# Head 0 of a patch-attention kernel: where its 1x1 results are written, in which order its units run, and when its keys are read

## The chip, the core and the metric

The kernel runs on one core of a Trainium2 chip. The metric is the device time of one execution in microseconds (us). TensorE is called PE here (PEld is its weight load), VectorE DVE, ScalarE ACT, GpSimd POOL and SyncE SP. DMAs are issued from three queues: SP's, ACT's and POOL's.

## The reference

An image x of 48 channels and 256 x 256 pixels goes through two layers. What matters here is the first part of the first layer.

```
x = x + L0(gn(x));  x = x + L1(gn(x))        # gn: group norm over 16 groups of 3 channels
L0(v):
    qkv = einsum('bchw,oc->bohw', v, w_qkv)   # 1x1 convolution, 48 -> 144 channels
    qkv = dwconv3x3(qkv, w_dw)                # each channel alone, 3x3 taps
    q, k, v = heads(unfold(split(qkv)))       # 4x4 patches (padding 4): 8 heads of 96 rows x 4356 patches
    q, k = l2norm(q), l2norm(k)               # over the 96 rows
    attn = softmax((q^T k) * temperature)     # 4356 x 4356 for each head
    out = w_proj @ fold(v @ attn)
```

The patches that lie in the padding are zero, so 4096 patches are computed and the others enter the softmax sum as a constant. L1 is a sum of three separable transforms over 64 x 64 windows; nothing of it is changed.

## The kernel before

Data flow of the first 260 us. The whole image is read into one tile `xr` (128 partitions, 128 rows of 256 pixels: the upper and lower half of the image in partitions 0 to 63 and 64 to 127). `bn_stats` on DVE and `group_stats` give the group norm, which is folded into the 1x1 weights `wq` (heads 0 and 1) and `wr` (heads 2 to 7) and a bias.

*1x1 results.* `mix(n)` (L626 on) computes the 1x1 convolution of heads 0 and 1, which have 36 channels, for four rows in each quarter of the image: 2 PSUM tiles of 1024 columns, each by 4 products on PE, moved out by ACT or DVE into one of four `oi` tiles that are 258 pixels wide with a zero at each end. Two DMAs, one on SP's queue and one on POOL's, store the 36 channels of both heads to the DRAM tensor `t1[0]`, whose rows are 258 wide. There are 16 such calls: 8 before the units, the other 8 between them (the table `behind`).

*Units.* A `Banded` unit is a quarter of the image rows (b = 0 to 3) for one of head 0's keys, queries and values (z = 1, 0, 2, in this order), so 12 units. Each does:

- `load`: 6 DMAs on SP's queue read its rows of `t1[0]`, with two rows of overlap, into a pad tile.
- `taps`: 6 products on PE with a banded matrix give the 3x3 convolution, in one PSUM tile of 96 x 1024.
- for keys and queries: `square` (ACT, from PSUM), `reduce` (DVE), `norm` (a product on PE), `root` (DVE, ACT, DVE), `scale` (DVE, from PSUM), `high` (ACT rounds to fp32r), `low` (DVE, the remainder), and two stores of 384 KB to the DRAM tensor `qkv0`, on ACT's and POOL's queues.
- for values: `copy` (ACT) and one store on ACT's queue.

The pads and the results lie in parts of `xr` whose pixels are no longer needed (`spare`). The order on every engine is the written one (`manual_schedule`): while unit k's first three products run, unit k-1 is normalised and scaled; only then come `high` of k-1, the other three products of k, `low` of k-1, `square` and `reduce` of k.

*Branch and keys.* Then comes `tc.If(large > 0)` (L717), whose body computes exact row maxima for large temperatures. With these inputs it is jumped over, and at its end SP waits for all DMAs that are under way. After it, the first queries and all 8 key tiles of head 0 (512 KB each, in four DMAs) are loaded over the three queues, then two value tiles. Attention (L477 logits, L804 exponentials, L838 weighted sums) follows; it works off head after head, while the units of the next head run beside it, and takes most of the time. Keys and queries are held as two fp32r parts, so a logits tile takes three products.

In the built program each DMA waits for the one that used its semaphore before: eight semaphores go round for POOL's queue, and eight for SP's and ACT's together.

Of the kernel before, what the change touches and what calls it, by code (L numbers as in the profile page):

```python
# [55 lines left out]
def conv_preact_kernel(  # L56
# [60 lines left out]
    early_only = taps.enter_context(tc.tile_pool(name="diag", bufs=1))  # L117
# [347 lines left out]
    def load_queries(qt, h, g):  # L465
        col = g * 256, (g + 1) * 256
        to = qt.bitcast(F32)
        for i in range(2):
            load(to[0:HD, i, :], h, i, 0, *col)
            load(to[HD:128, i, :], h, i, 0, *col, nc.sync, 0, 32)  # L470
            load(to[i * 64 : (i + 1) * 64, 2, :], h, i, 0, *col, nc.sync, 32)
# [26 lines left out]
    class Banded:  # L498


        def __init__(self, b, z, pad, spare):
            self.b, self.z, self.pad, self.spare = b, z, pad, spare

        def load(self):
            rows = t1[0][self.z * HE : (self.z + 1) * HE]
            for q in range(4):
                y = q * QR + self.b * BR
                nc.sync.dma_start(
                    out=self.pad[0 : BR * HE, q, :], in_=rows[:, y : y + BR, :].rearrange("c y x -> y c x")
                )  # L510
            for y in range(BR, BR + 2):
                y0 = self.b * BR + y
                nc.sync.dma_start(out=self.pad[y * HE : (y + 1) * HE], in_=rows[:, y0 : y0 + 3 * QR + 1 : QR, :])

        def taps(self, pool, half):

            if half == 0:
                self.ps = pool.tile([HD, 2, 512], F32, name="bps")
# [9 lines left out]
            self.acc = self.ps.rearrange("p i (q k x) -> p (i q) k x", q=2, k=KS)  # L528

        def square(self):  # L530
            self.sq = self.spare["sq"]
            nc.scalar.activation(
                self.sq.rearrange("p q n -> p (q n)"), self.ps.rearrange("p i n -> p (i n)"), AF.Square
            )

        def reduce(self):
            self.ss = small.tile([HD, 4, PX], F32, name="ss4")
            nc.vector.tensor_reduce(self.ss, self.sq.rearrange("p q (k x) -> p q x k", k=KS), AX.X, ALU.add)

        def norm(self, pool):  # L540
            self.pn = pool.tile([HD, BN], F32, name="pn4")
            nc.tensor.matmul(self.pn, lhsT=same4, rhs=self.ss.rearrange("p q x -> p (q x)"), start=True, stop=True)

        def root(self):
            n = small.tile([HD, BN], F32, name="n4")
            nc.vector.tensor_scalar_max(n, self.pn, 1e-24)
            nc.scalar.activation(n, n, AF.Sqrt)
            self.y = small.tile([HD, BN], F32, name="y4")
            nc.vector.reciprocal(self.y, n)
            if self.z == 0:  # L550
                nc.vector.tensor_scalar_mul(self.y, self.y, temp0)

        def scale(self):
            self.o = self.spare["o"]
            y = self.y.rearrange("p (q u x) -> p q u x", q=4, u=1).to_broadcast([HD, 4, KS, PX])
            nc.vector.tensor_tensor(self.o.rearrange("p k (q x) -> p q k x", q=4), self.acc, y, ALU.mult)

        def copy(self):
            self.o = self.spare["o"]
            nc.scalar.copy(self.o.rearrange("p k (q x) -> p q k x", q=4), self.acc)  # L560

        def high(self):
            self.oh = self.spare["oh"].bitcast(F32R)
            nc.scalar.copy(self.oh, self.o)

        def low(self):
            self.ol = self.spare["ol"].bitcast(F32R)
            nc.vector.tensor_sub(self.ol, self.o, self.oh.bitcast(F32))

        def store(self, i, eng):  # L570
            o = (self.o if i == 2 else (self.ol if i else self.oh).bitcast(F32))
# [3 lines left out]
    with tc.tile_pool(name="xn", bufs=1) as xnp, tc.tile_pool(name="cst", bufs=1) as cst, tc.tile_pool(  # L575
        name="oip", bufs=1
    ) as oip, tc.tile_pool(name="small", bufs=2) as small, tc.tile_pool(
        name="nps", bufs=1, space=PSUM
    ) as nps, tc.tile_pool(name="pw", bufs=1, space=PSUM) as pw, tc.tile_pool(name="pu", bufs=2, space=PSUM) as pu:
        zr = cst.tile([128, W + 2], F32, name="zr")  # L580
        nc.gpsimd.memset(zr, 0.0)
        for (h0, h1), t in zip(GROUPS, t1):
            for y in (0, H + 1):
                nc.gpsimd.dma_start(out=t[:, y, :], in_=zr[: (h1 - h0) * HC])
        xr = xnp.tile([PF, HALF, W], F32, name="xr")
# [29 lines left out]
        ois = [oip.tile([128, 2, OR, W + 2], F32, name=f"oi{i}") for i in range(4)]  # L615
        for t in ois:
            nc.gpsimd.memset(t[:, :, :, 0:1], 0.0)
            nc.gpsimd.memset(t[:, :, :, W + 1 : W + 2], 0.0)
        done = []

        def mix(n):

            ot = ois[len(done) % len(ois)]
            first = len(done) < AHEAD
            for i in range(0, OR, 2):
                of = pu if first and (len(done) * 2 + i // 2) % 3 else pw  # L626
                ps = of.tile([128, 2, 512], F32, name="pw", tag="bps" if of is pu else "pw")
                for c in range(2):
                    for s in range(2):
                        r = slice(s * 64, (s + 1) * 64)  # L630
                        y = c * QR + n * OR + i
# [3 lines left out]
                            rhs=xr[r, y : y + 2, :].rearrange("p a b -> p (a b)"),  # L635
# [3 lines left out]
                dst, src = ot[:, :, i : i + 2, 1 : W + 1], ps.rearrange("p s (a b) -> p s a b", a=2)  # L639
                if i and first:  # L640
                    nc.vector.tensor_scalar_add(dst, src, bias[:, 0:1])
                else:
                    nc.scalar.activation(dst, src, AF.Identity, bias=bias[:, 0:1])
            for c in range(2):
                to = t1[0][:, 1 : H + 1, :].rearrange("c (s y) x -> c s y x", s=2)
                to = to[:, :, c * QR + n * OR : c * QR + (n + 1) * OR, :]
                (nc.gpsimd if c else nc.sync).dma_start(out=to, in_=ot[c * 64 : c * 64 + M0])
            done.append(n)

        def spare(p, y, n=4):  # L650

            return xr[:p, y : y + n, :].rearrange("p a b -> p (a b)")

        AHEAD = 8
        pads = [spare(BI, y, 5)[:, : 4 * (W + 2)].rearrange("p (q x) -> p q x", q=4) for y in (60, 65, 70, 75)]
        spares = [
            {k: spare(HD, y).rearrange("p (q n) -> p q n", q=4) for k, y in ys.items()}
            for ys in (dict(sq=8, o=0, oh=16, ol=124), dict(sq=12, o=4, oh=80, ol=20))
        ]
        units = []  # L660
        for b in range(BQ):
            for z in (1, 0, 2):
                units.append(Banded(b, z, pads[len(units) % len(pads)], spares[len(units) % 2]))
        behind = {0: [7, 8], 1: [9, 10], 2: [11], 3: [12], 4: [13], 5: [14]}
        LEAD = 3
        with tc.manual_schedule():
            for n in [NQ1 - 1, *range(AHEAD - 1)]:
                mix(n)
                if n == 5:
                    for u in units[:LEAD]:  # L670
                        u.load()
            for k, u in enumerate([*units, None]):
                before = units[k - 1] if k else None
                scaled = before and before.z < 2
                if u:
                    u.taps(pu, 0)
                if scaled:
                    before.norm(nps)
                    before.root()
                    before.scale()  # L680
                for n in behind.get(k, ()):
                    mix(n)
                if scaled:
                    before.high()
                    before.store(0, nc.scalar)
                if u:
                    u.taps(pu, 1)
                    if k + LEAD < len(units):
                        units[k + LEAD].load()
                if scaled:  # L690
                    before.low()
                    before.store(1, nc.gpsimd)
                if u and u.z < 2:
                    u.square()
                    u.reduce()
                elif u:
                    u.copy()
                    u.store(2, nc.scalar)

    taps.close()  # L700
    attention = ExitStack()


    convolution = ExitStack()
    cv = convolution.enter_context(tc.tile_pool(name="cv", bufs=1, side="right"))
    NX = 3
    one = attention.enter_context(tc.tile_pool(name="one", bufs=2, space=PSUM))

    ots = [cv.tile([M1, 2, SR, W + 2], F32, name=f"ot{i}") for i in range(NOT)]

    def edges():

        for t in ots:
            nc.gpsimd.memset(t[:, :, :, 0:1], 0.0)
            nc.gpsimd.memset(t[:, :, :, W + 1 : W + 2], 0.0)

    with tc.If(nc.values_load(large) > 0):  # L717
        edges()
        with tc.tile_pool(name="sps", bufs=2, space=PSUM) as sps:
            for j in range(HALF // SR):  # L720
                w = Strip(j)
                w.load()
                w.run(sps)
                w.store()
        for h in range(1, NH):
            depthwise_all(h)
# [592 lines left out]
```

## Time and profile before

| | |
|---|---|
| median of 3 runs | 3505.17 us (3503.49 to 3512.53) |
| profiled execution, its own time | 3510.59 us |
| its span, first to last instruction | 3508.8 us |
| busy in the span: PE, DVE, ACT, POOL | 94%, 55%, 55%, 16% |
| mean granted clock of TensorE | 0.977 |
| image in, statistics done | 75.3 us |
| first 1x1 product | 75.9 us |
| first product of unit 0 | 112.35 us |
| last DVE operation of the units | 233.7 us |
| last of the waits at the branch ends | 239.9 us |
| logits run without a break from | 257.6 us |

The span is cut into views. The windows view gives, for stretches of the span, how long each engine was busy, the granted clock of TensorE, the share of the 16 DMA engines that was busy, and what they moved. The groups view gives, for a line of the kernel, the count and mean duration of its instructions. The timeline lists instructions in order of time, with what ended the idle time before them. "issue" means a wait for nothing that the profile shows.

### The profile page before, as it was taken

The numbers are of one execution on the slowest core, as the hardware profiler recorded it, in microseconds if no ns is written. First come the engines' busy times: TensorE is split into PE (matmuls) and PEld (weight loads), VectorE is DVE, ScalarE is ACT, GpSimd is POOL, SyncE is SP. The second block draws the span as 40 slices with busy tenths as digits, with TensorE's granted clock in tenths as the row PEclk, the third lists the DMA queues.
The fourth block names the chain that finished last, engine by engine and source line by source line (L and its number), as shares of the span: only waits on it lengthen the run. The fifth ranks groups of instructions, "written<-read, shape, count | busy, mean of one in ns | idle before, by whom it ended". The sixth has DMA issues, their size and how long they took to land.

```text
span 3508.8 us, 63563 instructions
## 1 busy us (share of the span) xinstructions
PE 3309.7 (94%) x25915; PEld 1845.4 (53%) x25915; DVE 1943.6 (55%) x2972; ACT 1924.5 (55%) x2876; POOL 566.4 (16%) x653
## 2 busy tenths in 40 slices
PE   2669999999999999999999999999999999987898
PEld 1225555555555555555555555555555555543676
DVE  7335763188628862886288528852885222228343
ACT  2326776566646664666466646664666444422343
POOL 2110121112211221122112211221122200003123
PEclk9889999999999999999999999999999999998899
DMA  6565666533323332333233423332333211139554
GB/s 150 152 160 152 179 171 172 157 95 94 95 73 85 94 95 77 82 95 94 78 81 94 95 77 81 94 96 77 81 95 96 71 49 51 27 73 311 130 151 117
DMA packets 220910, 376.94 MB, mean 107 GB/s; under 512 B 57468, under 2 KB 166860, under 8 KB 217634
## 3 DMA queue, kind: packets, MB, share of 16 engines
q1 hardware_dynamic: 174258, 245.33, 25.1%
q0 software_dynamic: 36768, 110.09, 13.7%
q10 hardware_dynamic: 9584, 17.37, 1.8%
q8 instruction: 207, 3.39, 0.4%
q14 instruction: 93, 0.76, 0.1%
HBM read 228.30 MB, written 144.17 MB: 106 GB/s over the span
## 4 chain that ended last, share of the span: by engine, by line
PE 86%; DMA 3%; DVE 1%; SPq 1%; issue 1%; ACT 0%; POOL 0%; POOLq 0%; ACTq 0%; DVEq 0%
PE big L477 40%; PE big L838 37%; PE pb L1209 2%; PE pa L1185 2%; PE pc L1228 2%; PE big L328 2%; DMA xs<-in_x_dram 2%; PE pst L781 1%; DMA x1s<-lxq 0%; DMA kt<-qkv 0%; SPq L1052 0%; DMA x1s<-pxt 0%; PE pps L1010 0%; DVE st L1019 0%; PE pn L387 0%
## 5 line engine op out<-in xcount | busy, mean ns | idle before, releaser
L804 ACT ACTIVATE e<-big,nmx 128x1024 f32<-128x1024 f32 x1024 | 1144.7, 1118 | 905.1 <-PE big L477 892.4
L477 PE MATMUL big<-kt,qt 128*128 128x512 f32 x6144 | 1455.8, 394 | 23.7 <-DMA kt<-qkv 23.7
L838 PE MATMUL big<-e,vn 128*32 128x512 f32 x12288 | 1350.1, 594 | 3.4 <-DVE vn L822 3.4
L477 PEld LDWEIGHTS big<-kt,qt 128*128 128x128 f32 x6144 | 1141.5, 188 | 364.0 <-issue 118.4
L852 DVE TENSOR_TENSOR oacc<-big,oacc 128x1024 f32<-128x1024 f32 x359 | 438.5, 1221 | 766.9 <-PE big L838 766.9
L838 PEld LDWEIGHTS big<-e,vn 128*32 128x32 f32 x12288 | 384.5, 110 | 886.0 <-issue 816.6
L368 DVE SCALAR_TENSOR_TENSOR acc<-pad,dwt,acc 126x1024 f32<-126x1024 f32 x560 | 718.7, 1283 | 15.3 <-issue 0.3
L431 POOL DMA_DIRECT2D qkv<-o x70 | 51.4, 734 | 1310.3 <-ACT o L415 1310.3
L818 DVE TENSOR_REDUCE zt<-zs 128x1 f32<-128x5 f32 x256 | 38.7, 151 | 316.2 <-ACT e L804 316.2
L425 POOL TENSOR_TENSOR ol<-o,oh 126x1024 fp32r<-126x1024 f32 x70 | 166.3, 2375 | 199.3 <-DVE ss L383 198.3
L804 ACT ACTIVATION_READ_ACCUMULATOR e<-big,nmx 128x1 f32 x1024 | 196.1, 192 | 0.0
L415 ACT COPY o<-acc 126x1024 f32<-126x1024 f32 x70 | 153.1, 2188 | 0.0
L1216 ACT COPY lyt<-pb 128x1024 f32<-128x1024 f32 x69 | 69.8, 1012 | 132.5 <-PE pb L1209 102.4
L335 ACT ACTIVATE ot<-big,bias 108x1024 f32<-108x1024 f32 x64 | 67.9, 1111 | 104.3 <-PE big L328 67.0
L1195 DVE COPY lzt<-pa 128x864 f32<-128x864 f32 (+1 forms) x69 | 67.5, 998 | 85.6 <-PE pa L1185 85.6
L872 POOL DMA_DIRECT2D os__70<-oacc x74 | 43.3, 593 | 415.4 <-DVE oacc L852 408.7
L364 ACT ACTIVATE acc<-pad,dwt 126x1024 f32<-126x1024 f32 x70 | 79.4, 1134 | 54.4 <-DMA pad<-t 54.4
L1209 PE MATMUL pb<-wsb,lzt 64*64 64x64 f32 x4608 | 86.1, 224 | 22.6 <-ACT lyt L1216 20.6
L379 ACT ACTIVATE sq<-acc 126x1024 f32<-126x1024 f32 x70 | 74.2, 1060 | 58.7 <-DVE acc L368 47.8
L1209 PEld LDWEIGHTS pb<-wsb,lzt 64*64 64x64 f32 x4608 | 79.2, 138 | 42.2 <-ACT lyt L1216 22.0
L453 POOL DMA_DIRECT2D kt<-qkv x28 | 14.7, 541 | 505.8 <-PE big L477 505.8
L1246 POOL DMA_DIRECT2D out_dram<-lrt x96 | 60.0, 632 | 199.4 <-DVE lrt L1242 151.1
(205 smaller groups left out, 1996.0 us busy)
## 6 DMA issues: line engine op xcount, KB each, us to landing
pad<-t SPq DMA_DIRECT2D x210, 254.0 KB
t<-ot SPq DMA_DIRECT2D x64, 435.4 KB
qkv<-oh POOLq DMA_DIRECT2D x70, 336.0 KB, 5.7
qkv<-ol POOLq DMA_DIRECT2D x70, 336.0 KB, 6.4
qt<-qkv SPq DMA_DIRECT2D x186, 96.0 KB
xs<-in_x_dram SPq DMA_DIRECT2D x64, 192.0 KB
out_dram<-lrt POOLq DMA_DIRECT2D x96, 128.0 KB, 3.1
qt<-qkv SPq DMA_DIRECT2D x186, 64.0 KB
```

Source lines behind the costliest of these rows:

```text
L328: nc.tensor.matmul(ps[:M1, s, :], lhsT=wr[r], rhs=self.xs[r, i : i + 2, :].rearrange("p a b -> p (a b)"), start=True, stop=True,)
L364: nc.scalar.mul(self.acc, self.pad[:, 0:KS, 0:W], dwt[:, self.h, 0:1])
L368: nc.vector.scalar_tensor_tensor(self.acc, self.pad[:, dy : dy + KS, dx : dx + W], dwt[:, self.h, tap : tap + 1], self.acc, ALU.mult, ALU.add,
L379: nc.scalar.activation(self.sq, self.acc, AF.Square)
L415: nc.scalar.copy(self.o.rearrange("p (a b) x -> p a b x", a=KS), self.acc.rearrange("p a (x b) -> p a b x", b=KS))
L425: eng.tensor_sub(self.ol, self.o, self.oh.bitcast(F32))
L477: nc.tensor.matmul(ps[:, i, :], lhsT=qt[:, r, q0 : q0 + 128], rhs=kts[2 * j + i][:, r // 2, :], start=(r == 0), stop=(r == 2),)
L804: nc.scalar.activation(e[:, j * 1024 : (j + 1) * 1024], ps.rearrange("p a b -> p (a b)"), AF.Exp, bias=nmx[:, b : b + 1], accum_out=zs[:, ...
L838: nc.tensor.matmul(ps[p * 32 : (p + 1) * 32, u, :], lhsT=vn[:, c * 32 : (c + 1) * 32], rhs=e[:, n * 512 : (n + 1) * 512], start=(i == 0), ...
L852: nc.vector.tensor_add(oaccs[h, pair], ps, old)
L1185: nc.tensor.matmul(pa[:, s, i * T3 * C : (i + 1) * T3 * C], lhsT=xq[r, y0 + i, xh * 128 : (xh + 1) * 128], rhs=csn[r], start=True, stop=True,)
L1209: nc.tensor.matmul(pb[s * WS : (s + 1) * WS, w, n * WS : (n + 1) * WS], lhsT=zts[u][r, t * C + b * 24 + q * 8 + s * 4 + i, :], rhs=wsb[r, ...
```

## The change

Nothing of what is computed changes. Five things do.

1. *1x1 results over x.* `mix` writes its results back into the pixels of `xr` that it has just read; the four `oi` tiles are gone, and all 16 calls come before the units. The two PSUM pools become one of three tiles.
2. *Stores.* `keep(h, n, count, engs)` stores one head at a time, 18 channels by 256 pixels of a row, without the zero columns. Head 0 goes during the products, in 36 DMAs, 18 each on SP's and POOL's queues. Head 1 follows in 16 DMAs on POOL's queue. The zero columns are written once, by two DMAs on POOL's queue ahead of all this: 36 channels x 257 places of two floats each (8 bytes).
3. *Units.* The convolution's PSUM tile is copied out at once by ACT (`copy`), and square, scale and remainder work in SBUF, in tiles of their own. `reduce` becomes two additions (96 x 512 and 96 x 256) in place of a `tensor_reduce`. A unit is spread over three steps: products, copy, square and reduce at step k; norm, root and scale at k+1; high, low and stores at k+2. Three pads in place of four; the store of `low` goes to SP's queue.
4. *Keys.* The tiles of the keys and queries take the place of `xr`, which is given up when the stores have read it. From step 7 on, POOL's queue loads keys 0 to 5, the first queries and two value tiles; keys 6 and 7 go on SP's queue after the last unit, and in the built program the second query tile stands just ahead of them.
5. *In the branch not taken,* the body's order and buffers change.

From the branch on, the instructions of each engine stand in the same order as before, without the loads that now come earlier.

```diff
+        def copy(self):
+            self.o = un.tile([HD, KS, BN], F32, name="o4", bufs=4)
+            nc.scalar.copy(self.o..., self.ps...)
         def reduce(self):
-            nc.vector.tensor_reduce(self.ss, self.sq..., AX.X, ALU.add)
+            nc.vector.tensor_add(self.sq[:, 0:2], self.sq[:, 0:2], self.sq[:, 2:4])
+            nc.vector.tensor_add(self.ss, self.sq[:, 0], self.sq[:, 1])
...
-                ot = ois[len(done) % len(ois)]
-                dst, src = ot[:, :, i : i + 2, 1 : W + 1], ps.rearrange("p s (a b) -> p s a b", a=2)
+                dst = xr.rearrange("p (s y) x -> p s y x", s=2)[:, :, y : y + 2, :]
+        def keep(h, n, count, engs):
+            p, y, m = h * HC, n * OR, count * OR
             for c in range(2):
-                (nc.gpsimd if c else nc.sync).dma_start(out=to, in_=ot[c * 64 : c * 64 + M0])
+                for s in range(2):
+                    to = s * HALF + c * QR + y + 1
+                    engs[s].dma_start(
+                        out=t1[0][p : p + HC, to : to + m, 1 : W + 1],
+                        in_=xr[c * 64 + p : c * 64 + p + HC, s * QR + y : s * QR + y + m, :],
+                    )
...
+            blank = st0.rearrange("p n s -> p (n s)")
+            nc.gpsimd.memset(blank, 0.0)
+            for y in range(0, H + 1, 192):
+                nc.gpsimd.dma_start(out=sides[:, y : y + n], in_=blank[:M0, : 2 * n]...)
+            mix(NQ1 - 1)
+            keep(0, NQ1 - 1, 1, both_queues)
+            for n in range(0, NQ1 - 1):
                 mix(n)
+                if n % 2:
+                    keep(0, n - 1, 2, both_queues)
                 if n == 5:
                     for u in units[:LEAD]:
                         u.load()
+            keep(0, NQ1 - 2, 1, both_queues)
+            for b in range(BQ):
+                keep(1, b * BR // OR, BR // OR, (nc.gpsimd, nc.gpsimd))
+            image.close()
+            for k in range(len(units) + 3):
+                u, near, far = (units[i] if 0 <= i < len(units) else None for i in (k, k - 1, k - 2))
+                near, far = (v if v and v.z < 2 else None for v in (near, far))
+                if u:
+                    u.taps(0)
+                    u.taps(1)
+                if near:
+                    near.norm()
+                if far:
+                    far.high()
+                    far.store(0, nc.scalar)
+                    far.low()
+                if u:
+                    u.copy()
+                    if u.z == 2:
+                        u.store(2, nc.scalar)
+                    else:
+                        u.square()
+                if near:
+                    near.root()
+                if u and u.z < 2:
+                    u.reduce()
+                if k + LEAD < len(units):
+                    units[k + LEAD].load()
+                if far:
+                    far.store(1, nc.sync)
+                if KEYS <= k < KEYS + BQ - 1:
+                    for m in range(2):
+                        load_key(0, (k - KEYS) * 2 + m, nc.gpsimd)
+                    if k == KEYS:
+                        load_query(0, 0, nc.gpsimd)
+                        for m in range(2):
+                            load_value(0, m, nc.gpsimd)
+                if k == len(units):
+                    for m in range(2):
+                        load_key(0, (BQ - 1) * 2 + m)
...
-        load_query(0, 0)
-        for m in range(NM):
-            load_key(0, m, (nc.scalar, nc.sync, nc.gpsimd)[m % 3])
         for m in range(2):
-            load_value(0, m)
             turn(0, m)
```

## The prediction

> **What bounds the kernel now.** I first read the windows view, 20 us at a time, because the change ends where attention begins.
>
> ```profile
> core 0: us, PE busy (x) PEld busy (x) DVE busy (x) ACT busy (x) POOL busy (x), PEclk, DMA share, GB/s
> 100.00:120.00 20.00, 8.34 (x26) 2.04 (x22) 2.57 (x2) 2.85 (x3) 1.22 (x2) 0.66 0.58 160
> 180.00:200.00 20.00, 16.82 (x51) 5.87 (x48) 10.28 (x10) 7.06 (x8) 1.29 (x2) 1.00 0.63 180
> 220.00:240.00 20.00, 7.89 (x15) 2.36 (x14) 9.70 (x9) 4.53 (x5) 1.28 (x2) 0.78 0.34 102
> 240.00:260.00 20.00, 5.18 (x11) 3.25 (x12) 0.06 (x1) 2.28 (x4) 5.03 (x12) 0.50 0.90 199
> 260.00:280.00 20.00, 20.00 (x111) 14.04 (x113) 1.60 (x7) 14.64 (x27) 0.00 (x0) 0.95 0.58 151
> ```
>
> From 260 us on PE is full and stays the bound to the end. Up to then no engine is full and the DMA engines are half busy: a chain of waits bounds the units. In 240 to 260 us only the DMA engines work, on the keys. From the branch on both programs have the same instructions in the same order, so the whole effect is one date: when logits run without a break, 257.63 us now. I call it A. A gain before A is a gain of the kernel, since PE has no later slack that would swallow it.
>
> The groups between 60 and 265 us price the units:
>
> ```profile
> L538 DVE TENSOR_REDUCE ss<-xr 96x256 f32<-96x1024 f32 x8 | 15.2, 1900 | 49.4 <-ACT xr L532 49.4
> L549 DVE RECIPROCAL y<-n 96x256 f32<-96x256 f32 x8 | 14.0, 1749 | 3.9 <-ACT n L547 3.9
> L568 DVE TENSOR_TENSOR xr<-xr 96x1024 fp32r<-96x1024 f32 x8 | 9.8, 1221 | 16.3 <-ACT xr L564 16.3
> L556 DVE TENSOR_TENSOR xr<-bps,y 96x1024 f32<-96x1024 f32 x8 | 9.8, 1220 | 0.3
> L564 ACT CAST xr<-xr 96x1024 fp32r<-96x1024 f32 x8 | 8.3, 1038 | 13.0 <-DVE xr L556 13.0
> L532 ACT ACTIVATE xr<-bps 96x1024 f32<-96x1024 f32 x8 | 8.2, 1019 | 14.6 <-PE bps L521 13.4 <-ACT xr L564 1.3
> ```
>
> DVE and ACT wait for each other in turn: 49.4 us for the square, 16.3 for the rounding, 13.0 for the scale. Last, the timeline around the branch, and DMA rows:
>
> ```profile
> 234.17 0.56 ACTq L572 DMA_DIRECT2D qkv<-xr  x1
> 240.11 0.06 DVE L787 MEMSET border<- 128x1 f32 x1 [6.41 <-SPq L717]
> 240.42 3.37 SPq L446 DMA_DIRECT2D qt<-qkv  x6
> 257.63 8.02 PE L477 MATMUL big<-kt,qt 128*128 128x512 f32 x25 [2.90 <-DMA kt<-qkv]
> ```
>
> ```profile
> q10 hardware_dynamic: 6714, 6.83, 11.8%
> ...
> qkv<-oh POOLq DMA_DIRECT2D x70, 336.0 KB, 5.7
> ...
> qkv<-o POOLq DMA_DIRECT2D x70, 168.0 KB, 3.5
> ```
>
> The last DVE operation of the units ends at 233.7 us. Then the last store lands, the branch is passed at 239.9, and the keys take 17 us: 24 us from 233.7 to A.
>
> **The change part by part.** I date each step in the profiled execution.
>
> *1x1 products.* In the stretch without stalls DVE moves out a tile at 84.65, 86.41, 88.13 and 89.85 us, so one call (two tiles, ACT and DVE) takes 1.73 us. The waits for stores of `oi` (ACT 5.7 us, DVE 3.0 us) cannot come, as the results stay in place. The first call's DVE tile ends at 85.9; 15 more end at 85.9 + 15 x 1.73 = 112 us. PE takes no unit before that. Unit 0 starts at 112.35 now, so this by itself gains nothing at the start, but the 8 calls that now lie between the units are gone from them.
>
> *Zero columns: new, and not in the trace.* 36 x 257 = 9252 runs of 8 bytes, issued after the statistics (72.7 us) and the POOL memset, moving from some 76 us. The nearest row is the store in 256-byte runs: 672 runs land in 3.5 us and 1344 in 5.7, so 3.3 ns a run, together 31 us. Low end: in the first 15 us 479 small packets of POOL's queue take 5.0% of 16 engines, 25 ns of an engine each, 9252 x 25 / 16 = 14 us. High end: each run costs what a 1 KB packet costs on ACT's queue, 11.8% of 16 x 205 us over 6714 = 58 ns, on 12 of the 16 engines if three partitions go to each, 45 us. I take the 256-byte row, the nearest in kind (many short runs to DRAM on this queue), and add 6 us for the first stores of `keep`, 1.8 MB at 286 GB/s (180 at a share of 0.63). The columns are then written at S = 76 + 31 + 6 = 113 us (low 91, high 127).
>
> The page "DMA: Bandwidth & Descriptors" of the Trainium skill (Specifications) says that below 512 bytes a DMA reads, modifies and writes, which speaks against these writes; its rule on how many engines share a DMA ("Why a DMA increments its semaphore by 16 and not by 1") would put an 18-partition store on 9 engines, and 2304 rows of SP's half at 58 ns on 9 would take 15 us instead of 8. No run yet shows either.
>
> *Who waits for S.* On POOL's queue the stores of calls 4 and 5 take the semaphores of the two column DMAs, so they, and all stores behind them, wait for S. Unit 0's loads on SP's queue wait for the columns and those stores; behind these loads stand SP's remaining stores. From S: two issues of 0.61 us and a landing of 4.8 us (the shortest of `t<-oi`), then six load issues (4 x 0.60 + 2 x 0.42 = 3.2 us) and some 2 us until the last has landed: unit 0 starts at T0 = S + 11 = 124 us, or at some 115 if S is early, since PE is at the 1x1 products until 112.
>
> *Units.* Now 9.3 us each (126.9 to 233.7 us for the last eleven and a half). The new order splits the chain over three steps; I follow ACT and DVE through three successive units:
> - products of a key: ACT rounds (1.04), issues (0.6), copies (1.01), squares (1.02); DVE subtracts (1.22), adds (0.64 + 0.35, by size from the 1.22 of 1024 columns): 3.7 us, ACT bound.
> - products of a query: copy, square, root (0.42) on ACT, then reciprocal 1.75, scale 1.22, additions 1.0 on DVE: 6.6 us.
> - products of a value: round 1.04 (started under the additions), issue, copy, issue, root, then reciprocal 1.75, temperature 0.35, scale 1.22: 6.3 us.
>
> That is 16.6 us for three. PE: a unit is 12 product instructions (144 for 12 units), 0.43 us apart at full clock (208.64 us: 18 in 7.94 us), 5.2 us, and 0.7 for a norm: 3 x 5.2 + 2 x 0.7 = 17.0 us for three. The norm of the query waits for its additions, 6.6 us after its products, while the value's end 5.9 after them: 0.7 us of idle. So PE sets 17.7 us for three units. From T0 the last value's products end at 16.3 + 3 x 17.7 = 69.4 us, 2 us more for a slow clock at the start; then norm (1.4 us with its wait), maximum, root, reciprocal, temperature, scale (4.2 us), round and subtract (2.3 us): 79 us. Where PE had paused 1.8 us, six products took 4.43 and 4.29 us (204.03, 226.88) instead of 2.6, and the granted clock of such stretches is 0.66 and 0.78: each such pause costs 1.8 us more.
>
> *DMA beside the units.* This cover may be too thin. After T0 there remain: loads 3.9 MB, stores of units 7.7, SP's rest of head 0 1.3, head 1 3.6 (4.7, less what POOL moves from S to T0), keys 0 to 5, queries and values 3.9: 20.4 MB. At 221 GB/s (199 at a share of 0.90, the key loads) to 286 that is 71 to 92 us; at 250, 82. It is as long as the chain, and everything must have landed before the branch is passed. I take 84 us and two pauses of PE, 4 us: the units end at 124 + 88 = 212.
>
> *Tail.* 24 us now. New: SP issues the last store, 6 query DMAs and 8 key DMAs, about 15 x 0.57 = 8.6 us; the last lands some 3 us later; the branch ends; 8 transposes stand before the logits, 1 us: 13 us. A = 212 + 13 = 225. The exponent table load (1.28 us on ACT) lies under the first products, as now.
>
> *Free edits.* `reduce`'s two additions are in the sum. POOL's memset and issues have no reader but the DMAs told. The longer body behind the branch isn't run; a jump cost PE 3.9 us at 227, while DVE was still at work, and PE again arrives early. If that cover went, 4 us.
>
> *Sum.* 257.6 - 225 = 32.6 us less. 3510.6 - 32.6 = 3478; the profiled execution stands 5.4 us above the median of the runs, so 3472.6, say 3473.
>
> **The rivals.**
> - *Columns cheap, DMA ample.* S = 91, T0 = 115, 79 us of units: A = 115 + 79 + 13 = 207, a gain of 51 us, 3455. For it: POOL's small packets at 25 ns. Against: 20.4 MB in 79 us is 258 GB/s without a pause.
> - *DMA becomes the bound.* With few partitions in each store and three queues mixed, 185 GB/s (what 160 to 200 us shows now) give 110 us: A = 247, gain 11 us, 3494. Pauses of PE do the same: one in each unit is 12 x 1.8 = 22 us. For it: head 1 and the keys are now crowded in. Against: 185 was not taken at a full share.
> - *Keys still late.* POOL's key loads stand behind head 1's stores in its queue; if they land no earlier than now after the units, the tail is 24 us again and the gain 22, 3484. The step would not do what it says.
> - *Slower: the columns decide.* If an 8-byte write costs twice the 1 KB packet, 116 ns on 12 engines, they take 89 us, S = 171, T0 = 182. Units 79, tail 13: A = 274, 16 us slower, 3521. It decides from T0 = 257.6 - 92 = 166, S = 155, on: 79 us less the 6 of the stores, 73 us for 9252 runs, 7.9 ns a run, 2.4 times the 256-byte row. For it: no write so short is in the trace. Against: less data per run.
>
> **How the numbers follow.** 0.3% or 10.5 us is about what a measurement of this kernel tells from no change. Chances: forecast (with the late keys) 0.50, cheap columns 0.15, DMA or clock bound 0.18 (0.10 of it above 10.5 us), slower 0.17 (0.13 beyond 10.5 us, the rest within). Faster 0.50 + 0.15 + 0.10 = 0.75; same 0.08 + 0.04 = 0.12; slower 0.13. The range goes from 3453, all of the cheap case, to 3508, with the DMA bound and the near end of the slower one in it. The likeliest case alone has 3462 (T0 = 115, 9 us earlier, and one pause fewer) to 3487 (S = 127, 14 us later).
>
> **What would show it.** After: DVE and ACT move 32 tiles with no wait for `t`; POOL's column DMAs land near 113 us (about 91 or beyond 160 in the rivals); unit 0's products at 124; a unit every 6 to 7.5 us with DMA share above 0.8 and a granted clock near 1; the SP wait at the branch near 223; logits without a break at 225. I am wrong if the first products start beyond 166, if the units' pace is still 9 us, or if keys are still awaited after the branch.

## The result, and the profile after

The changed kernel takes 3486.47 us (median of 7 runs, 3480.56 to 3492.75); the kernel before, on the same chip, takes 3503.49 (7 runs, 3497.86 to 3512.53). The ratio is 0.9952, with a 95% interval of 0.9936 to 0.9968. It is faster by 17.0 us, about half of the 32.6 us that were forecast and inside the range.

The windows view of the changed kernel, 20 us at a time, with the columns as before (length; busy time of PE, weight loads, DVE, ACT, POOL; granted clock, DMA share, GB/s):

```profile
100.00:120.00 20.00, 20.00 (x188) 6.56 (x184) 14.39 (x12) 12.29 (x12) 6.94 (x12) 0.98 0.68 161
120.00:140.00 20.00, 19.00 (x64) 6.92 (x56) 8.96 (x11) 7.66 (x8) 9.62 (x15) 1.00 0.91 177
140.00:160.00 20.00, 0.13 (x1) 0.00 (x0) 5.55 (x6) 2.47 (x3) 4.09 (x6) 0.54 0.95 191
160.00:180.00 20.00, 10.22 (x17) 3.76 (x18) 0.00 (x0) 1.75 (x2) 1.36 (x3) 0.60 0.66 168
180.00:200.00 20.00, 19.00 (x47) 7.38 (x46) 11.73 (x14) 8.26 (x10) 8.46 (x15) 1.00 0.88 235
240.00:260.00 20.00, 15.80 (x56) 12.36 (x55) 1.00 (x6) 10.29 (x19) 0.29 (x4) 0.81 0.23 68
```

The gap of 240 to 260 us is gone: PE was busy for 5.18 of these 20 us and is now for 15.80. But a new gap stands at 140 to 170 us. PE is idle in it, DVE and ACT finish their last instructions at 151.6 us, and until 160 us the DMA engines are full: 0.95 of them busy, for only 191 GB/s. The timelines name it. First PE (start, length, line, and in brackets the idle time before and its releaser), then SP's own queue, then the two lines of DVE and ACT that matter:

```profile
122.33 10.54 PE L522 MATMUL bps<-bpad,band 108*96 108x512 f32 x24
133.14 5.31 PE L522 MATMUL bps<-bpad,band 108*96 108x512 f32 x12
169.78 13.55 PE L522 MATMUL bps<-bpad,band 108*96 108x512 f32 x24 [29.65 <-DMA bpad<-t]
248.28 14.50 PE L477 MATMUL big<-kt,qt 128*128 128x512 f32 x50 [4.20 <-ACT e L828]
```

```profile
123.28 28.05 SPq L663 DMA_DIRECT2D t<-xr  x10
151.42 13.32 SPq L509 DMA_DIRECT2D bpad<-t  x4
```

```profile
94.21 0.06 DVE L811 MEMSET border<- 128x1 f32 x1 [12.02 <-DMA t<-st]
247.02 1.11 ACT L828 ACTIVATE e<-big,nmx 128x1024 f32<-128x1024 f32 x1 [6.67 <-SPq L751]
```

Units 0 to 2 run from 122.3 on, and then PE waits 29.65 us for the rows of unit 3. SP had ten stores of head 0 to issue ahead of these loads. It took 28.05 us to issue them, and then 13.32 us for the first four loads. The trace shows no wait for a semaphore there: the semaphore instructions ahead of these stores took 28 ns each, while a single issue took 0.27 to 6.56 us, with a median of 2.48. From unit 3 on the pace is good: nine units up to the last DVE operation at 233.5 us. That is the date it had before (233.7). So **the units end where they did, and all of the gain is in the tail behind them**: A = 248.3 against 257.6.

The memset of `border` is a second loss. It belongs to attention, and in the kernel before it ran behind the branch (at 240.11 us). In the changed program as built it stands on DVE ahead of the 1x1 results, and it waits for the column transfers. The sentence ahead of the prediction that each engine's order from the branch on is the same as before overlooks this. DVE is idle for 12.02 us, and it has moved out the last 1x1 result at 123.8 us instead of 112.

The groups between 60 and 265 us, to set beside those of before:

```profile
L557 DVE RECIPROCAL y<-n 96x256 f32<-96x256 f32 x8 | 14.0, 1749 | 13.9 <-ACT n L555 13.9
L568 DVE TENSOR_TENSOR o<-o,oh 96x1024 fp32r<-96x1024 f32 x8 | 9.8, 1222 | 4.7 <-ACT oh L565 4.4
L544 DVE TENSOR_TENSOR sq<-sq 96x512 f32<-96x512 f32 x8 | 5.5, 685 | 37.9 <-ACT sq L539 37.9
L565 ACT CAST oh<-o 96x1024 fp32r<-96x1024 f32 x8 | 8.4, 1045 | 26.1 <-DVE o L561 26.1
```

The instructions cost what was forecast (two additions of 0.685 and 0.42 us for a reduction of 1.90). DVE still waits 37.9 us for the squares, but 28.8 of them are one wait, in the gap from 151.6 us on.

In the two profiled executions (3510.6 and 3492.2 us of device time) the first product of `weigh` lies at 275.87 and 263.62 us, 12.3 us apart. The other 6 of the 18 us between them appear later, between 330 and 1032 us. The trace of before has there a pause of 2.1 us for `xs`, with the granted clock at 0.68 in 470 to 480 us, which the trace after has not. Whether that comes from the change was not tested. Below, **W is the date of the first `weigh` product** (L838 before, L862 after): it is easier to compare than A, because A moves when a few logits run ahead of a last wait.

### The profile page after: what moved, and what is told of

The parts are those of the page before. It is cut to its first block, busy times and chain, and to the rows that moved or that the text cites. A ratio compares the mean times of both kernels' runs of the same rounds, so it can differ in the third digit from the quotient of the medians.

```text
span 3490.4 us, 63589 instructions
## 1 busy us (share of the span) xinstructions
PE 3288.8 (94%) x25915; PEld 1843.4 (53%) x25915; DVE 1947.2 (56%) x2988; ACT 1923.3 (55%) x2876; POOL 591.3 (17%) x682
## 4 chain that ended last, share of the span: by engine, by line
PE 88%; DMA 2%; ACT 1%; DVE 0%; SPq 0%; issue 0%; POOL 0%; ACTq 0%; POOLq 0%; DVEq 0%
PE big L477 41%; PE big L862 38%; PE pb L1229 2%; PE pa L1205 2%; PE big L328 2%; PE pc L1248 2%; DMA pot<-os__70 1%; PE pst L805 1%; DMA pxt<-in_x_dram 1%; DMA lxq<-in_x_dram 1%; SPq L1072 0%; PE pn L387 0%; DMA kt<-os__70 0%; PE big L1030 0%; ACT lyt L1236 0%
## 5 line engine op out<-in xcount | busy, mean ns | idle before, releaser
L862 PE MATMUL big<-e,vn 128*32 128x512 f32 x12288 | 1350.3, 594 | 3.4 <-DVE vn L846 3.4
L862 PEld LDWEIGHTS big<-e,vn 128*32 128x32 f32 x12288 | 384.7, 110 | 886.0 <-issue 817.0
L522 PE MATMUL bps<-bpad,band 108*96 108x512 f32 x144 | 66.3, 616 | 29.7 <-DMA bpad<-t 29.7
```

The source lines that it names most:

```text
L862: nc.tensor.matmul(ps[p * 32 : (p + 1) * 32, u, :], lhsT=vn[:, c * 32 : (c + 1) * 32], rhs=e[:, n * 512 : (n + 1) * 512], start=(i == 0), ...
```

## The experiments

My first theory, T, was that the stores' traffic crowds out unit 3's loads, head 1's 4.7 MB above all. Rivals: the wait of `border` is the main loss (B); SP's queue order (Q); the form of the stores, 18 partitions (P); the DMA engines have a fixed amount of work, and delaying a part only moves the wait (R). The table holds every run; each ratio is taken to runs of the kernel before on the same chip. "unit 3" is its first product and PE's wait ahead of it; "end" is the end of the last DVE operation of the units; "rate" is GB/s from about the first store of head 0 (within 1.6 us of it) to that end. All dates are in us, from one profile of each run.

| run | median us | ratio to before, 95% | unit 0 | unit 3 (wait) | end | rate | W |
|---|---|---|---|---|---|---|---|
| before | 3503.5 | | 112.4 | | 233.7 | | 275.9 |
| the change | 3486.5 | 0.9952 (0.9936 to 0.9968) | 122.3 | 169.8 (29.7) | 233.5 | 186 | 263.6 |
| e1_border | 3477.2 | 0.9923 (0.9909 to 0.9938) | 111.9 | 156.0 (26.3) | 219.7 | 195 | 249.8 |
| e2_head1_later | 3481.9 | 0.9943 (0.9928 to 0.9957) | 120.8 | 170.2 (31.6) | 232.8 | 186 | 259.8 |
| e3_both | 3473.4 | 0.9912 (0.9895 to 0.9929) | 110.4 | 157.9 (29.7) | 221.2 | 192 | 248.3 |
| e5_keys_late | 3496.9 | 0.9977 (0.9965 to 0.9989) | 118.8 | 166.3 (29.8) | 229.5 | 162 | 268.0 |
| e6_together | 3480.3 | 0.9941 (0.9926 to 0.9956) | 138.6 | 164.3 (5.1) | 228.0 | 195 | 251.8 |
| e7_in_time | 3473.1 | 0.9917 (0.9901 to 0.9933) | 111.5 | 144.6 (15.3) | 220.7 | 193 | 249.5 |
| e8_gated | 3480.7 | 0.9935 (0.9918 to 0.9951) | 110.3 | 138.4 (10.4) | 229.1 | 181 | 258.2 |
| e9_together_border | 3470.5 | 0.9908 (0.9893 to 0.9923) | 128.9 | 154.4 (5.9) | 217.7 | 201 | 242.0 |
| e10_together_in_time | 3469.7 | 0.9904 (0.9887 to 0.9922) | 131.7 | 151.6 (0) | 223.4 | 193 | 247.2 |
| e11_early | 3465.9 | 0.9894 (0.9876 to 0.9913) | 127.0 | 152.3 (5.0) | 215.4 | 205 | 239.4 |
| e12_early_gated | 3469.5 | 0.9901 (0.9881 to 0.9920) | 113.3 | 153.5 (10.3) | 216.3 | 204 | 240.4 |
| e13_split | 3489.4 | 0.9950 (0.9934 to 0.9966) | 134.5 | 174.9 (20.5) | 238.0 | 175 | 262.4 |

### `border` out of the way

```diff
-        border = ao.tile([128, 1], F32, name="border")
-        nc.vector.memset(border, math.log(NBORDER))
+    border = const.tile([128, 1], F32, name="border")   # at the start
+    nc.vector.memset(border, math.log(NBORDER))
```

> Only the constant `border` is moved: another pool, written at the start, so that VectorE has no wait for the zero columns among the 1x1 results (12.0 us of idle VectorE in the changed kernel). The 1x1 products then end near 112 us instead of 123.8. Theory T (the 29.65 us that TensorE waits for unit 3's loads are set by the traffic of the stores behind the 1x1 products): the stores start some 10 us earlier, but unit 3 is still held; its wait stays over 25 us, and A, the date from which the logits run without a break (248.3 in the changed kernel), comes 3 to 10 us earlier. Rival B (the wait for the columns is what halved the gain): A comes the full 12 us earlier, near 236, and the time is 12 us under the changed kernel's.

PE's timeline in this run:

```profile
111.93 10.54 PE L524 MATMUL bps<-bpad,band 108*96 108x512 f32 x24
156.01 13.54 PE L524 MATMUL bps<-bpad,band 108*96 108x512 f32 x24 [26.28 <-DMA bpad<-t]
234.50 15.40 PE L479 MATMUL big<-kt,qt 128*128 128x512 f32 x54 [4.18 <-ACT e L828]
```

The 1x1 products end at 112 us, as the prediction had it, and A comes 13.8 us earlier (234.5), the whole of the stall: rival B's number. T was right that unit 3's wait stays (26.3 us) and wrong that it would swallow the gain. The burst of stores starts earlier with the 1x1 results, and the wait at its end shifts with it. The median falls by 9.3 us, where B had 12.

### Head 1's stores later

```diff
-            for b in range(BQ):
-                keep(1, b * BR // OR, BR // OR, (nc.gpsimd, nc.gpsimd))
-            image.close()
+                # in unit step k; image.close() in step 6
+                if 2 <= k < 2 + BQ:
+                    keep(1, (k - 2) * BR // OR, BR // OR, (nc.gpsimd, nc.gpsimd))
```

> Only the stores of head 1's rows are moved: four each in unit steps 2 to 5 on POOL's queue, instead of sixteen ahead of the units. Theory T: unit 3's loads no longer share the DMA engines with 4.7 MB of head 1; TensorE's wait before unit 3 falls from 29.65 to 8 to 18 us, the units end 10 to 20 us before 233.5, A lies at 228 to 238, the time 10 to 20 us under the changed kernel's. Rival Q (SP's own queue holds the loads: ten stores of head 0's rest stand ahead of them): the wait stays over 24 us and A within 5 us of 248. Rival R (the DMA engines' total work up to the end of the units decides, in whatever order): the wait shrinks, but the later units wait longer, and they still end at 230 to 234, A 246 to 249.

> Both edits, of `border` and of head 1's stores. Theory T: the two gains add: the 1x1 products end near 112, unit 3 waits 8 to 20 us, the units end at 202 to 218, A at 217 to 233, the time 15 to 31 us under the changed kernel's. Rival B: as with the edit of `border` alone, near 236. Rival R: the units end 0 to 6 us before 233, A at 242 to 248.

Unit 3's wait stayed at 31.6 and 29.7 us, and A in the first run at 247.3: Q's signs. But this says nothing against T, because the stores had not moved in time. POOL's timeline, of the changed kernel and of this one:

```profile
123.03 5.19 POOL L663 DMA_DIRECT2D t<-xr  x8 [2.62 <-ACT xr L655]
```

```profile
121.51 7.21 POOL L663 DMA_DIRECT2D t<-xr  x11 [2.62 <-ACT xr L655]
```

POOL runs no part of a unit, so a later place in the program gave it nothing to wait for, and it issued the stores as early as before, the last at 153.5 us (159.2 in the changed kernel). With `border` moved too, A is 235.8 and W 248.3, against 234.5 and 249.8 with `border` alone: nearly the same run again. To hold the stores back they need something that waits:

```diff
+                    gate = un.tile([HD, 1], F32, name="gate")
+                    nc.gpsimd.tensor_copy(gate, u.o[:, 0, 0:1])
                     keep(1, (k - 2) * BR // OR, BR // OR, (nc.gpsimd, nc.gpsimd))
```

> The deferral of head 1's stores did not happen in the run that only moved them in the program: POOL has nothing else to wait for and issued them at the same dates as before. Here one copy of a column of the unit's result on POOL ahead of each four holds them back until units 2 to 5 have run; `border` is moved too. Theory T: without head 1's 4.7 MB between 112 and 150 us TensorE's wait before unit 3 falls from 29.7 to 8 to 18 us, A from 235.8 to 216 to 228. Rival Q (SP's ten stores ahead of the loads take their time whatever else runs): the wait stays over 24 us, A at 232 to 237. Rival R (full DMA engines): the wait shrinks, later units wait, A at 230 to 238.

```profile
129.14 0.18 POOL L726 COPY gate<-o 96x1 f32<-96x1 f32 x1 [15.73 <-ACT o L534]
129.38 2.73 POOL L665 DMA_DIRECT2D t<-xr  x4
146.85 0.18 POOL L726 COPY gate<-o 96x1 f32<-96x1 f32 x1 [14.74 <-ACT o L534]
```

```profile
138.44 7.24 PE L524 MATMUL bps<-bpad,band 108*96 108x512 f32 x12 [10.39 <-issue]
158.18 7.06 PE L524 MATMUL bps<-bpad,band 108*96 108x512 f32 x12 [3.07 <-DMA bpad<-t]
169.93 8.55 PE L524 MATMUL bps<-bpad,band 108*96 108x512 f32 x12 [4.26 <-DMA bpad<-t]
```

Now T's mechanism is shown, against Q: without head 1's traffic SP issues its ten stores in 11.0 us instead of 23, and unit 3's wait falls from 29.7 to 10.4 us. But T's gain does not come. The stores fall among the loads of later units, four further waits of 1.9 to 4.3 us come up, each with a slower start of the products, and the units end at 229.1, 7.9 us **later** than with the long wait. That the wait moves is R's sign. A, at 244.1, is beyond R's 230 to 238, though, and the DMA engines were not full (shares of 0.49, 0.58 and 0.69 at 120 to 130, 140 to 150 and 160 to 170 us). The waits view of this run shows another cause beside it (who waited, for what: us in total, times, longest):

```profile
ACT o L534 <- DMA bpad<-t: 26.8, 4, 8.9
```

By this view ACT's copies of the units' results waited for loads of SP's queue, 26.8 us in all; in `e3_both` it is 0.7 us. The copy needs no load, but ACT issues a store just ahead of it (at 169.61 us for the copy at 170.27, after the longest wait), and SP's and ACT's transfers share eight semaphores in the built program. That this ties them is my reading of the order; no run tests it. How much of the 7.9 us comes from it, and how much from busy DMA engines, stays open.

### Head 0's late stores behind unit 3's loads

```diff
-                if n % 2:
+                if n % 2 and n < 10:
                     keep(0, n - 1, 2, both_queues)
-            keep(0, NQ1 - 2, 1, both_queues)
...
+                if k < 2:                    # after units[k + LEAD].load()
+                    keep(0, 10 + 2 * k, 2 + k, both_queues)
```

> To the edits of `border` and of head 1's place in the program, a third is added: head 0's last five stores (4-row steps 10 to 14) come behind the loads of units 3 and 4 on SP's queue, instead of ahead of them; POOL's share of them still issues at once, since nothing on POOL waits for a unit. Theory Q (unit 3's loads wait because SP issues them only after its ten stores, 23 us of issuing): TensorE's wait before unit 3 falls from 29.7 to under 15 us, and A from 235.8 to 220 to 230. Rival R (the DMA engines are full from 112 on, and whatever is late only changes its place): the wait moves to a later unit, A at 232 to 238.

> As the run with both heads stored together and `border` moved, and with the stores of the last five 4-row steps behind the loads of units 3 and 4 on SP's queue. Theory Q: unit 3 no longer waits 5 us, and units 1 and 2 lose nothing: A 3 to 8 us earlier than without this edit. Rival R: the stores delay units 6 to 11 by as much, A within 2 us.

Unit 3 waits 15.3 us instead of 29.7, and then units 4, 5 and 7 wait 1.8, 1.4 and 4.8. The end is at 220.7 against 221.2, and A at 235.4: R's numbers. ACT was held here too:

```profile
ACT o L534 <- DMA bpad<-t: 18.4, 2, 14.2
ACT n L557 <- DMA t<-xr: 8.8, 1, 8.8
```

With both heads stored together (next) the edit makes the units end later, at 223.4 against 217.7, and W comes 5.2 us later; neither Q nor R had that. The medians, 3469.7 and 3470.5, do not differ. The gain that Q forecast came in neither run.

### Both heads in one store

Here one part of the change is undone: rows of heads 0 and 1 leave together, 36 partitions to a transfer, in head 0's places.

```diff
-            p, y, m = h * HC, n * OR, count * OR
-                        out=t1[0][p : p + HC, to : to + m, 1 : W + 1],
-                        in_=xr[c * 64 + p : c * 64 + p + HC, ...],
+                        out=t1[0][:, to : to + m, 1 : W + 1],
+                        in_=xr[c * 64 : c * 64 + M0, ...],
...
-            for b in range(BQ):
-                keep(1, b * BR // OR, BR // OR, (nc.gpsimd, nc.gpsimd))
```

> One part of the change is undone: heads 0 and 1 are stored together, 36 partitions in a transfer, on the queues and at the places of head 0's stores, and the pass of head 1 is left out. Theory T: the same bytes are ahead of unit 3's loads, so its wait stays at 25 to 35 us; unit 0 starts 3 to 10 us later, since twice the bytes lie ahead of its loads; A 248 to 258, the time 0 to 10 us over the changed kernel's. Rival P (it is the form of 18 partitions on POOL's queue, 94 ns per KB between 124 and 152 us against 63 on SP's, that makes the stores slow): with 36 partitions they move faster, unit 3 waits under 20 us, and A falls to 235 to 243.

> Heads 0 and 1 stored together (A 233.9 in that run), and `border` moved. If both causes are separate, the 5.8 us that TensorE lost to VectorE's wait for the columns come off as well, with the pause of VectorE behind it: A at 222 to 229, the time 4 to 12 us under that run's 3480. If the loads of unit 0, behind twice the bytes, hide the earlier products: unit 0 still starts at 135 to 139, and A stays at 231 to 235.

Unit 0 starts later, with twice the bytes ahead of it, and unit 3's wait shrinks to 5 us. T had 25 to 35 us for it, which did not come; a wait under 20 was P's sign. But much of the wait has only gone over to unit 0: unit 3 itself starts 5.5 us earlier, and the units end 5.5 us earlier, at 228.0. With `border` moved as well, unit 0 starts at 128.9 and A is 223.6, as expected if the two causes are separate. The units end at 217.7, only 2.0 us before the run with `border` alone; so head 0 first against both heads together is worth little up to there. Another 5.8 us are gained behind: W lies 24.3 us after the units' end, not 30.1. SP's timeline, of the run with `border` alone and of this one:

```profile
220.60 3.37 SPq L448 DMA_DIRECT2D qt<-qkv  x6
224.01 4.95 SPq L448 DMA_DIRECT2D kt<-qkv  x8
```

```profile
218.40 5.50 SPq L448 DMA_DIRECT2D kt<-qkv  x8
```

The six loads of the second query group stand ahead of the last keys in the first and among the units' stores in the second. I did not ask for it: the scheduler placed them so in each of the six runs that store both heads together, and in none of the others. So this part of the gain was luck of the order. No run changes this order alone. It is also not all of the 5.8 us: in `e3_both`, with the late order, W lies 27.1 us after the end. There the 54 logits products from A on took 12.5 us at a granted clock of 1.00, in the run with `border` alone 15.4 us at 0.80.

To test P, each store was issued as two of 18 partitions, in the same order of rows:

```diff
+                    for p in (0, HC):
+                        engs[s].dma_start(
+                            out=t1[0][p : p + HC, to : to + m, 1 : W + 1],
+                            in_=xr[c * 64 + p : c * 64 + p + HC, ...],
+                        )
```

> As the run with both heads together and `border` moved (A 223.5, 3470.5 us), but each store of 36 partitions is issued as two of 18, one behind the other, on the same queue and in the same order of rows. Rival P (the form of 18 partitions is what moves slowly): the stores take 85 to 100 ns of a DMA engine per KB on POOL's queue, as in the changed kernel, instead of about 70; A 231 to 238 and the time 6 to 14 us higher. If it is the order (head 1's rows in a pass of their own, behind head 0's) that costs: A stays at 221 to 227.

The units end 20.3 us later, and A (243.9) and the time (18.9 us more) lie beyond both forecasts. But the run is not clean. The waits of SP's queue between 137 and 171 us:

```profile
SPq L666 <- DMA qkv<-oh: 17.4, 2, 12.8
```

SP's later stores waited for a store of ACT's queue, which ACT issued only at 153.7 us, in the step of unit 2. In the program as built, SP's and ACT's transfers take eight completion counters in turn, and with more transfers the turns meet differently; this reading is from the program's order, and no run tests it. From 150 to 155 us no DMA engine moved anything. SP's waits there add up to 18.2 us, so most of the 20 us are likely these. P's own sign did not come: from 94 to 124 us the stores on POOL's queue took 71 ns of a DMA engine per KB (0.531 of 16 engines for 3.59 MB), against 78 in the run with 36 partitions (0.686 for 4.24 MB). Something else shows where SP's stores run alone. The windows of this run, and of the run with 36 partitions:

```profile
140.00:145.00 5.00, 5.00 (x13) 1.95 (x12) 0.80 (x2) 2.06 (x2) 0.00 (x0) 1.00 0.53 152
150.00:155.00 5.00, 3.42 (x9) 1.06 (x7) 4.87 (x6) 1.60 (x2) 0.00 (x0) 1.00 0.00 0
```

```profile
138.00:146.00 8.00, 8.00 (x21) 3.26 (x20) 3.83 (x5) 2.55 (x4) 0.00 (x0) 1.00 0.72 214
```

A queue of 18-partition stores keeps 0.53 of the engines busy and moves 152 GB/s, one of 36 partitions 0.72 and 214. This agrees with the Trainium skill, "DMA: Bandwidth & Descriptors" (Why a DMA increments its semaphore by 16 and not by 1): by its rule a store of 18 partitions is spread over 9 of 16 engines (a share of 0.56) and one of 36 over 12 (0.75). In the changed kernel two queues together filled the engines (0.95), so fewer engines for one queue were not what bound it there. The form slows a queue that runs alone; that it caused the changed kernel's loss is not shown. How much of the 20.3 us here is the form's stays open.

### The keys late again

```diff
-                    # in the unit steps, on POOL's queue: keys 0 to 5, queries, values
-                        load_key(0, (k - KEYS) * 2 + m, nc.gpsimd)
+        load_query(0, 0)                     # behind the units
+        for m in range(NM):
+            load_key(0, m, (nc.scalar, nc.sync, nc.gpsimd)[m % 3])
```

> Of the changed kernel one part is undone: keys, queries and values of head 0 are loaded behind the units, on three queues, as in the kernel before. Priced by the prediction: the tail between the last unit's VectorE work and A goes from 14.8 back to 24 us, A from 248.3 to 256 to 259, the time 8 to 10 us over the changed kernel's 3486.5. Rival R (the loads of the keys take engine time from the units): the units end 4 to 10 us earlier than 233.5 without them, A at 247 to 253, the time 0 to 4 us over.

Each came true in part: A, at 249.7, and the units' end are R's; the time, 10.4 us over, is nearly the price's 8 to 10. Without key loads beside them the units end at 229.5, 4.0 us earlier, and the way from there to W is 38.5 us instead of 30.1, 8.4 us longer. W is 4.4 us later. The intervals of the two ratios overlap by no more than 0.0003. Loading the keys early is worth 4 to 10 us of the change's 17.

### A version that beats both

```diff
-                if n % 2:
+                if n < 4 and n % 2 or n > 4 and n % 2 == 0:
                     keep(0, n - 1, 2, both_queues)
-                if n == 5:
+                if n == 4:
+                    keep(0, n, 1, both_queues)
                     for u in units[:LEAD]:
                         u.load()
+                    # second run only: POOL's later stores wait for unit 0's rows
+                    gate = un.tile([BI, 4, 1], F32, name="gate")
+                    nc.gpsimd.tensor_copy(gate, units[0].pad[:, :, 0:1])
```

> As the run with both heads together and `border` moved; the rows that units 0 to 2 need are stored after five 4-row steps instead of six, and their loads come one step earlier. If what counts is the date at which unit 0's loads can go: unit 0 at 123 to 127 instead of 128.9, A at 218 to 222. If the DMA engines' work decides: A 222 to 226.

> As the run before, and POOL's later stores wait, by one copy of a column on POOL, until unit 0's rows have landed, so that these loads have fewer stores beside them and the stores fall into the stretch in which the engines were at 0.45 (124 to 140 us). If that stretch can be filled: unit 0 at 112 to 120, A at 208 to 217. If the stores only come late for units 3 to 5: unit 0 early, a wait of over 8 us before unit 3, A 220 to 228.

With both heads together and `border` moved, the first run has the lowest median of all: 3465.9 us, 0.9894 of before (0.9876 to 0.9913), some 20 us under the change. Its interval overlaps those of the next three, so it is not told apart from them. Unit 0 starts at 127.0, and the logits run from 221.2 but for one gap of 0.24 us: the first of the two cases. The gate did what it was for, with unit 0 at 113.3, and brought nothing: units 2 and 3 then waited 8.3 and 10.3 us, the end is 216.3 against 215.4, and A is 222.1. That is the second case: the wait moved again.

**What the runs say together.** Where nothing interrupts units 3 to 11, they take 62.6 to 63.8 us from the first product of unit 3 to the end (ten rows of the table). This chain needs unit 3 to start early *and* its loads to flow. The 26 MB between the first store and the end moved at 175 to 205 GB/s whatever their order (22 MB at 162 without the keys), and an early unit 3 (138, 145 us) was paid back. This fits R, but R is not shown as it stands: over these stretches the DMA engines' share was about 0.67 to 0.8, with 0.44 from 120 to 130 us in `e9_together_border`, so they were not full throughout, and in two of its runs ACT was held by transfers. What moved the end was to start the burst earlier (`border`, 13.8 us), and little else: 2 to 5.5 us from larger stores, 2.3 from earlier loads.

## Why the prediction was half right

- **1x1 products: the pace was right, the end was not.** A call took 1.72 us (forecast 1.73), and no result waited for a store. They ended at 123.8 instead of 112, because I followed only instructions that the change touches. DVE's order as built had an untouched one, `border`, behind a new wait. The run without it ended at 112.
- **Zero columns: mis-sized.** They were issued from 73.6 us on and had landed at 94 (forecast 113, of which 6 us were for the first stores; the low end, 91, left these out): 9252 runs in some 20 us, 2.2 ns a run, where I took 3.3 from the 256-byte row. The row of POOL's small packets, my low end, came closer. The Trainium skill's page "DMA: Bandwidth & Descriptors" (Specifications) tells of a read and write-back under 512 bytes. That was no guide to the cost here: a run of 8 bytes came cheaper than one of 256, which lies under 512 as well. Whether such a write-back took place no run shows.
- **T0 = 124: 122.3 measured, by luck: two errors cancel.** The columns were 19 us early, and `border` held the 1x1 products back by 12. Unit 0 started when PE was through with these products (122.3; 111.9 without the hold).
- **The units' chain: right.** My sum gives 79 - 17.7 = 61.3 us for the last nine units; ten rows of the table show 62.6 to 63.8.
- **DMA beside the units: this step failed.** "I take 84 us and two pauses of PE, 4 us: the units end at 124 + 88 = 212." From unit 0's start to the end were 111 us. The bytes were nearly right (21.9 MB, that is 197 GB/s in the window from 122.3 to 233.5 us; forecast 20.4). The rate was not: those 197 GB/s against 243, which is 20.4 MB in 84 us. The time was lost ahead of unit 3, since from 180 to 220 us 235 to 248 GB/s moved. I had let it run on the share that stood free before. But at a share of 0.91 to 0.95 the mix of stores moved 177 to 191 GB/s. I had even rejected the right figure with "185 was not taken at a full share". And I let bytes and units overlap from the first moment, though ten stores stood in SP's queue ahead of unit 3's loads, which I had written down.
- **The rival "DMA becomes the bound" named it**: 110 us, A = 247, gain 11, against 111, 248.3 and 9.3 measured. It had a chance of 0.18. The time fell by 17.0 us, though, and not by its 11: 12.3 us stand at W, and no run explains the rest. That the total came out at half the forecast is in part luck.
- **Tail: right.** 13 us forecast, 14.8 measured, 24 before; undoing it lengthened the way to W by 8.4 us. The last wait in it is ACT's, 6.67 us for SP to pass the branch; 17 logits products ran before it.
- **A gain before A is a gain of the kernel: right to within some 6 us.** Measured from before, the median and W moved by amounts that differ by -5.5 to 1.5 us in the change and its twelve variants. Differences of a few us between runs are not settled by their dates: `e10_together_in_time` has W 5.2 us later than `e9_together_border` and the same median.

## What to carry to other kernels

Price a transfer by the rate at a full share in the stretch it moves into, not by the share that looks free; and when the engines are nearly full, expect that a delayed transfer may only move the wait, as it did here. Read the built order of every engine for instructions that the diff does not touch: a memset of one column cost 9.3 us, more than any single reordering of the stores brought. A transfer placed later in the program on a queue that waits for nothing is not later.

## What the runs showed of the hardware that I had not expected

- With full DMA engines the issue of a transfer is itself slow: SP's 18-partition stores took 2.48 us each (median) between 123 and 151 us in the changed kernel and 0.79 in `e8_gated`, without head 1's stores beside them.
- 8-byte writes to DRAM, 9252 of them in two transfers, landed in 17.3 and 19.1 us; the trace has them as 240 packets, 0.09 MB at a share of 0.415.
- A store on SP's queue waited 12.8 us for one on ACT's that touches other data. By the program's order it is the completion counters, which the two queues share, that tie them; no run tests this.
